# Layer-0 attention output with the head dimension on partitions: four-quadrant values, norm sums by a product with ones, norm applied behind the output product

## The chip, the cores and the metric

The kernel runs on one NeuronCore of a Trainium2 chip. The core has TensorE (PE, matrix products; its weight loads are listed as PEld), VectorE (DVE), ScalarE (ACT), GpSimd (POOL) and SyncE (SP, which issues most DMAs), each working through its own instructions in order. The metric is the device time of one execution in microseconds, lower is better; the median of several executions is compared.

## The reference

x is 64 sequences of 32 tokens with 256 features. Two layers each do x = x + attention(conditioning(x)) and x = x + mlp(conditioning(x)). The change lies in layer 0's attention, which has 16 heads of 128 (H, DK, DV) and 64 memory slots per head (M):

```python
A = jnp.where(mask, jnp.einsum('bhtd,bhjd->bhtj', q, k) * scale, 0.0)
ok = enz * jnp.einsum('bhtj,bhjm->bhtm', A, es)
qv = jax.nn.softmax(ok, axis=-1)
W2 = jnp.where(mask, jnp.einsum('bhtm,bhjm->bhtj', qv * enz, es), 0.0)
o = jnp.einsum('bhtj,bhjd->bhtd', W2, v)
o_n = o * jax.lax.rsqrt(jnp.mean(o * o, axis=-1, keepdims=True) + EPS) * g_norm_weight
o_g = o_n * (g * jax.nn.sigmoid(g))
return o_g.reshape(B, T, H * DV) @ Wo.T
```

q, k, v and g are projections of the conditioned tokens, with rotary embedding on q and k; es is exp of the clipped slot logits and enz the reciprocal of its running sum.

## The kernel before

The attention runs as a software pipeline over 32 steps: four groups of four heads (hq) times eight groups of 256 tokens (q, eight sequences each). `turn(n)` writes out by hand, once per n from -1 to 33, the order in which the pieces of neighbouring steps are issued, and this order is the order on every engine. In turn n, step n+1 gets its slot exponentials (`slots_exp`), rotated queries and keys (`project_qk`, two pairs of heads, the second pair later in the turn) and running sums (`cumsum`); step n gets `scores`, `attend`, `weigh`, the value and gate projections (`project_vg`) and `turn_qe`; step n-1 gets `mix`, `values`, `norm`, `gate` and `turn_og`; and step n-2 gets `leave`.

Lines that matter here: line 779 is the q/k projection on TensorE. Lines 790 and 791 multiply it on DVE with cosine and sine into the tiles ra and rb, and lines 793 and 794 combine these on POOL into qT and kT. Line 841 is the slot logits, 843 their exp on ACT, 848 the clip on DVE. Line 889 is the scores, 896 their mask on DVE (tile aT). Line 910 is the attend product, 918 gives `ok` on DVE, 923 its maximum, 927 the softmax exponentials on ACT. Line 864 is the running sum and 873 its reciprocal on DVE. Line 936 is `qe` = qv * enz on POOL, 950 its turning by TensorE (transposes against an identity), 954 the copy of it on ACT. Line 967 is `mix` and 975 its mask on DVE (tile w2T).

The output side: `values` (line 992) has 64 tokens on partitions and 128 columns of d in each product, two heads' parity in two PSUM banks (po). Line 1001 squares each head's 128 columns on ACT and sums them (eight instructions, each followed by an accumulator read). `norm` adds the epsilon term on DVE (line 1008) and raises to the power -1/2 on POOL (line 1010). `gate` (line 1022, eight DVE instructions) multiplies by the norm factor, a number per partition, and by Silu(g). `turn_og` (line 1032, eight transposes on TensorE, copied by ACT at lines 1036 and 1039) brings d onto the partitions, and `leave` (line 1047) multiplies with Wo, the four heads adding up in PSUM, and line 1052 adds the result to x. The epsilon term e2 is made by DVE at line 943 in `weigh`.

PSUM has eight banks, all from one pool; a product waits until the bank that it is given has been read out. Most work tiles have two buffers, some one.

Beside the attention the loop carries other work. `ahead()`, called twice in a turn, takes the next step of `preparing`: rounding the last layers' weights on DVE (lines 226 to 240 for f1, f3 and f2, then lines 196 to 204 for thirteen rows) alternating with short steps that turn the rounded rows on TensorE (line 256). `tabulating` issues table gathers on POOL (line 433). The wo weights of each head group are scaled on DVE (line 687) every eighth turn. The later stages (layer 0's mlp and layer 1, chunk by chunk) follow the loop; the first of their chunks is woven into the last turns by `more`.

Of the kernel before, what the change touches and what calls it, by code (L numbers as in the profile page):

```python
# [9 lines left out]
F32 = mybir.dt.float32  # L10
I32 = mybir.dt.int32
AF = mybir.ActivationFunctionType
ALU = mybir.AluOpType
AX = mybir.AxisListType

P = 128
B = 64
T = 32
D = 256
# [57 lines left out]
def mk_kernel(  # L77
# [10 lines left out]
    nc = tc.nc  # L88
    MULT, ADD, SUB, MAX, MIN = ALU.mult, ALU.add, ALU.subtract, ALU.max, ALU.min
# [5 lines left out]
    def bank():  # L95
        return psum.tile([P, 512], F32, tag="ps", name="ps")
# [11 lines left out]
    ident = const("ident")  # L108


    xq = [keep.tile([P, 2, D], F32, tag=f"x{q}", name=f"x{q}") for q in range(8)]
# [23 lines left out]
    ones = keep.tile([P, P], F32, tag="ones", name="ones")  # L135
    mhalf = keep.tile([P, 8], F32, tag="mhalf", name="mhalf")
# [511 lines left out]
    with ExitStack() as s1:  # L648
        p1 = s1.enter_context(tc.tile_pool(name="p1", bufs=1))
        work = s1.enter_context(tc.tile_pool(name="work", bufs=2))  # L650
# [117 lines left out]
        def at(i):  # L768
            hq, q = steps[i]
            return hq, q, weights[hq], hsT[q // 2], (q % 2) * 256, state[i]  # L770
# [30 lines left out]
        def by_parity(ap):  # L801
            return ap.rearrange("p (r e d) -> p r e d", r=2, e=2)

        def project_vg(i, which):
            hq, q, w, hs, lo, s = at(i)
            wt = w[2 if which == "v" else 3]
            for gi in range(2):
                ps = bank()
                for c in range(2):
                    nc.tensor.matmul(  # L810
                        ps, lhsT=hs[:, c, lo + gi * P : lo + (gi + 1) * P], rhs=wt[:, c, :],
                        start=(c == 0), stop=(c == 1),
                    )
                t = work.tile([P, 512], F32, tag=which, name=which, bufs=2)
                if which == "v":
                    nc.scalar.copy(t, ps)
                else:
                    to, of = by_parity(t), by_parity(ps)
                    nc.scalar.activation(to[:, :, 0, :], of[:, :, 0, :], AF.Silu)
                    for half in range(2):  # L820
                        here, there = slice(half * 64, half * 64 + 64), slice(64 - half * 64, P - half * 64)
                        nc.scalar.activation(to[here, :, 1, :], of[there, :, 1, :], AF.Silu)
                s[which, gi] = t

        E32 = float(np.exp(np.float32(32.0)))

# [23 lines left out]
        def quarters(product):  # L850


            for e in range(2):
                for at in range(2):
                    out = at ^ e
                    product(e, slice(64 * at, 64 * at + 64), slice(64 * out, 64 * out + 64))
# [76 lines left out]
        def weigh(i):  # L933
            s = state[i]
            qe = work.tile([P, 512], F32, tag="qe", name="qe", bufs=1)
            nc.gpsimd.tensor_tensor(
                qe.rearrange("p (k e m) -> p e k m", k=4, e=2),
                s["qv"].rearrange("p (e k) m -> p e k m", e=2),
                s["enz"].rearrange("p e (k m) -> p e k m", k=4), MULT,
            )  # L940

            e2 = work.tile([P, 8], F32, tag="e2", name="e2")
            nc.vector.scalar_tensor_tensor(e2, s["rs"], 1e-5, s["rs"], MULT, MULT)
            s["qe"], s["e2"] = qe, e2

        def turn_qe(i):
# [32 lines left out]
            s["w2T"] = w2T  # L979

        def values(i):
            s = state[i]
            f = work.tile([P, 8], F32, tag="f", name="f")
            s["f"] = f
            po = [bank(), bank()]
            s["po"] = po
            for k in range(4):
                gi, pr = k // 2, k % 2

                def product(e, rows, out):  # L990
                    h = pr * 2 + e
                    nc.tensor.matmul(  # L992
                        po[e][out, k * P : (k + 1) * P], lhsT=s["w2T"][rows, e, k, :],
                        rhs=s["v", gi][rows, h * P : (h + 1) * P], start=True, stop=True,
                    )

                quarters(product)
            for e in range(2):
                for k in range(4):
                    sq = work.tile([P, P], F32, tag="sq", name="sq", bufs=1)  # L1000
                    nc.scalar.activation(  # L1001
                        sq, po[e][:, k * P : (k + 1) * P], AF.Square,
                        accum_out=f[:, e * 4 + k : e * 4 + k + 1],
                    )

        def norm(i):
            s = state[i]
            nc.vector.scalar_tensor_tensor(s["f"], s["f"], 1.0 / P, s["e2"], MULT, ADD)  # L1008
            f2 = work.tile([P, 8], F32, tag="f2", name="f2")
            nc.gpsimd.tensor_tensor(f2, s["f"], mhalf, ALU.pow)  # L1010
            s["f2"] = f2

        def gate(i):

            s = state[i]
            f2 = s["f2"]
            for gi in range(2):
                s["og", gi] = work.tile([P, 4, P], F32, tag="og", name="og")
            for k in range(4):
                for e in range(2):  # L1020
                    gi, h = k // 2, k % 2 * 2 + e
                    nc.vector.scalar_tensor_tensor(
                        s["og", gi][:, h, :], s["po"][e][:, k * P : (k + 1) * P],
                        f2[:, e * 4 + k : e * 4 + k + 1], s["g", gi][:, h * P : (h + 1) * P], MULT, MULT,
                    )

        def turn_og(i):
            s = state[i]
            for gi in range(2):
                ps = bank()  # L1030
                for h in range(4):
                    nc.tensor.transpose(ps[:, h * P : (h + 1) * P], s["og", gi][:, h, :], ident)  # L1032
                t = work.tile([P, 4, P], F32, tag="ogT", name="ogT")
                to = t.rearrange("p (r e) t -> p r e t", e=2)
                of = ps.rearrange("p (r e t) -> p r e t", r=2, e=2)
                nc.scalar.copy(to[:, :, 0, :], of[:, :, 0, :])
                for half in range(2):
                    here, there = slice(half * 64, half * 64 + 64), slice(64 - half * 64, P - half * 64)
                    nc.scalar.copy(to[:, :, 1, here], of[:, :, 1, there])
                s["ogT", gi] = t  # L1040

        def leave(i):
            hq, q, w, hs, lo, s = at(i)
            ps = bank()
            for gi in range(2):
                for h in range(4):
                    nc.tensor.matmul(  # L1047
                        ps[:, gi * D : (gi + 1) * D], lhsT=s["ogT", gi][:, h, :], rhs=w[4][:, h, :],
                        start=(h == 0), stop=(h == 3),
                    )  # L1050
            xf = xq[q].rearrange("p g f -> p (g f)")
            nc.vector.tensor_tensor(xf, ps, xf, ADD)
            s.clear()

        def turn(n):

            def on(i, f, *a):
                if 0 <= i < len(steps):
                    f(i, *a)

            def more(*at):

                if n in at:
                    next(beyond)

            def ahead():
                if 2 <= n < len(steps):
                    next(preparing, None)

            N = len(steps)  # L1070
            on(n + 1, slots_exp)
            on(n, scores)
            more(N)
            on(n - 1, mix)
            on(n + 1, slots_clip)
            more(N - 1)
            on(n - 2, leave)
            more(N - 1)
            on(n + 1, project_qk, "q", 0)
            on(n + 1, project_qk, "k", 0)  # L1080
            if n < 2:
                condition(n + 2)
            on(n - 1, values)
            on(n, attend)
            on(n + 1, cumsum)
            more(N)
            on(n - 1, norm)
            on(n + 1, project_qk, "q", 1)
            on(n + 1, project_qk, "k", 1)
            on(n - 1, gate)  # L1090
            on(n, weigh)
            on(n, project_vg, "v")
            on(n, project_vg, "g")
            if n < 2:
                low_rank(n + 2)
            if n < 1:
                gather_cond(n + 3)
            if n == 1:
                small_tables()
            ahead()  # L1100
            more(N - 1)
            on(n, turn_qe)
            on(n - 1, turn_og)
            more(N)
            ahead()

# [570 lines left out]
```

## Time and profile before

| | |
|---|---|
| median of 3 runs | 1453.79 us (1450.05 to 1453.99) |
| the profiled execution's own time | 1451.43 us |
| its span | 1449.7 us |
| granted TensorE clock, mean | 0.992 |
| attention loop (first slot logits to last output product) | about 22 to 834 us |
| a turn of the loop, steady state | 23.34 to 23.62 us |

A page of the profile gives busy times, then the chain of work that ended last, followed back from the last instruction, then groups of instructions by line. A row of a group names the tile written and the tiles read, partitions x elements, how often, the busy time and the mean time of one, and the idle time of the engine before them with what ended it. A TensorE product in fp32 appears as two records, a transpose as one.

### The profile page before, as it was taken

The page shows a single profiled execution, that of the slowest core. Times are in us where ns is not written, and L with a number is a line of the kernel's source. Part 1 is how long each engine was busy: PE and PEld are TensorE (multiplying, and loading weights), DVE is VectorE, ACT ScalarE, POOL GpSimd, SP SyncE. Part 2 cuts the span into 40 slices and gives each one's busy share as a digit, 9 for nine tenths or more (in the row PEclk, how much of TensorE's full clock was granted, in tenths as well). Part 3 has the DMA queues.
Part 4 walks back from the last instruction along what each step waited for, and adds up shares of the span by engine and source line. Part 5 has one row for each costly group of instructions (what it writes and reads, how often), then busy time and mean ns, then how long its engine had stood idle before and what let it go on. Part 6 is the DMA issues. An engine that isn't in the chain of part 4 may idle for free.

```text
span 1449.7 us, 39390 instructions
## 1 busy us (share of the span) xinstructions
PE 1399.7 (97%) x16552; PEld 1086.2 (75%) x16552; DVE 829.9 (57%) x1879; ACT 614.1 (42%) x2014; POOL 577.2 (40%) x650
## 2 busy tenths in 40 slices
PE   5899999999999999999999999999999999999996
PEld 3666777776767677767777788888887878788874
DVE  1566686867677776766565323363636262635554
ACT  1355665656575756565655512130312121212121
POOL 3423367777533333333445141524251606060320
PEclk9999999999999999999999999999999999999999
DMA  6201001321221000100001161313131304040220
GB/s 172 61 2 67 5 16 20 77 47 33 35 66 36 23 6 15 38 12 1 13 14 44 38 115 52 98 49 92 39 102 34 107 17 123 6 116 23 67 74 15
DMA packets 101625, 71.41 MB, mean 49 GB/s; under 512 B 71429, under 2 KB 88965, under 8 KB 101449
## 3 DMA queue, kind: packets, MB, share of 16 engines
q0 software_dynamic: 15744, 38.03, 9.5%
q1 hardware_dynamic: 82504, 26.34, 7.6%
q10 hardware_dynamic: 3200, 4.52, 1.0%
q8 instruction: 131, 2.15, 0.6%
q14 instruction: 46, 0.37, 0.1%
HBM read 64.54 MB, written 6.29 MB: 49 GB/s over the span
## 4 chain that ended last, share of the span: by engine, by line
PE 91%; DMA 3%; SPq 2%; DVE 2%; issue 1%; ACT 1%; POOL 0%; ACTq 0%; DVEq 0%
PE ps L779 16%; PE ps L810 15%; PE ps L1047 8%; PE ps L507 8%; PE ps L1398 5%; PE ps L578 4%; PE ps L553 3%; PE ps L1438 3%; PE ps L597 3%; PE ps L992 2%; PE ps L521 2%; PE ps L889 2%; PE ps L1206 2%; PE ps L1032 2%; SPq L276 1%; PE ps L967 1%
## 5 line engine op out<-in xcount | busy, mean ns | idle before, releaser
L433 POOL DMA_INDIRECT we<-in_ew,at x64 | 61.1, 955 | 277.5 <-DVE h L1405 203.7
L1001 ACT ACTIVATE sq<-ps 128x128 f32<-128x128 f32 x256 | 71.1, 278 | 211.6 <-PE ps L992 204.4
L793 POOL TENSOR_TENSOR qT<-ra,rb 128x256 f32<-128x256 f32 x64 | 46.6, 728 | 272.6 <-DVE rb L791 272.5
L1047 PE MATMUL ps<-wo,ogT 128*128 128x256 f32 x512 | 120.6, 389 | 6.1 <-DVE aT L896 6.1
L779 PE MATMUL ps<-hsT,wq 128*128 128x256 f32 x512 | 126.4, 390 | 0.0
L779 PE MATMUL ps<-hsT,wk 128*128 128x256 f32 x512 | 122.2, 382 | 0.0
L790 DVE TENSOR_TENSOR ra<-ps,ct 128x512 f32<-128x512 f32 x128 | 87.4, 683 | 49.9 <-PE ps L779 44.9
L810 PE MATMUL ps<-wv,hsT 128*128 128x512 f32 x256 | 115.2, 593 | 0.0
L810 PE MATMUL ps<-wg,hsT 128*128 128x512 f32 x256 | 115.1, 592 | 0.0
L1047 PEld LDWEIGHTS ps<-wo,ogT 128*128 128x128 f32 x512 | 95.8, 192 | 20.9 <-DVE aT L896 6.6
L779 PEld LDWEIGHTS ps<-hsT,wq 128*128 128x128 f32 x512 | 95.5, 192 | 18.3 <-issue 5.8
L873 DVE RECIPROCAL enz<-ps 128x256 f32<-128x256 f32 x64 | 107.5, 1721 | 2.7 <-PE ps L864 2.7
L779 PEld LDWEIGHTS ps<-hsT,wk 128*128 128x128 f32 x512 | 98.3, 192 | 13.7
L1010 POOL TENSOR_TENSOR f<-f,mhalf 128x8 f32<-128x8 f32 x32 | 53.1, 1660 | 133.5 <-DVE f L1008 133.5
L810 PEld LDWEIGHTS ps<-wg,hsT 128*128 128x128 f32 x256 | 48.6, 190 | 61.2 <-issue 54.3
L791 DVE TENSOR_TENSOR rb<-ps,ct 128x512 f32<-128x512 f32 x128 | 87.0, 680 | 0.0
L927 ACT ACTIVATE qv<-ok,nmx 128x64 f32<-128x64 f32 x256 | 85.0, 336 | 1.3 <-DVE nmx L923 1.3
L810 PEld LDWEIGHTS ps<-wv,hsT 128*128 128x128 f32 x256 | 48.6, 190 | 47.6 <-issue 45.9
L1398 PE MATMUL ps<-guT,y3T 128*128 128x352 f32 x256 | 79.5, 464 | 0.5 <-ACT y3T L395 0.5
L529 DVE TENSOR_TENSOR hT<-ps,sg 128x256 f32<-128x256 f32 x64 | 24.2, 419 | 96.9 <-ACT sg L528 96.9
L896 DVE SCALAR_TENSOR_TENSOR aT<-ps,ct 128x256 f32<-128x256 f32 x64 | 24.1, 419 | 85.6 <-PE ps L889 85.6
L433 POOL DMA_INDIRECT ag<-alora,at x56 | 53.4, 954 | 49.3 <-DVE at L431 39.3
(233 smaller groups left out, 3056.4 us busy)
## 6 DMA issues: line engine op xcount, KB each, us to landing
x<-in_x SPq DMA_DIRECT2D x8, 256.0 KB
wq<-in_wqT SPq DMA_DIRECT2D x16, 128.0 KB
wk<-in_wkT SPq DMA_DIRECT2D x16, 128.0 KB
wv<-in_wvT SPq DMA_DIRECT2D x4, 512.0 KB
wg<-in_wgT SPq DMA_DIRECT2D x4, 512.0 KB
wo<-in_woT SPq DMA_DIRECT2D x4, 512.0 KB
row<-in_wgu ACTq DMA_DIRECT2D x11, 128.0 KB
out<-res SPq DMA_DIRECT2D x5, 256.0 KB
```

The lines of the kernel that those rows point to most:

```text
L433: nc.gpsimd.indirect_dma_start(out=to, out_offset=None, in_=table, in_offset=bass.IndirectOffsetOnAxis(ap=at, axis=0))
L507: nc.tensor.matmul(ps[:, i * 256 : (i + 1) * 256], lhsT=mlp[name, k // 4][:, j, part], rhs=c["xT"][:, j, :], start=(i == 0 and j == 0), st ...
L578: nc.tensor.matmul(ps[:, i * 256 : (i + 1) * 256], lhsT=wt[:, j, k * P : (k + 1) * P], rhs=yT[:, j, :], start=(j == 0), stop=(j == 1),)
L779: nc.tensor.matmul(ps[:, half * 256 : (half + 1) * 256], lhsT=wt[:, c, half * 256 + pr * P : half * 256 + (pr + 1) * P], rhs=hs[:, c, lo : ...
L790: nc.vector.tensor_tensor(by_t(a.rearrange("p h t -> p (h t)")), by_t(ps), cosb, MULT)
L791: nc.vector.tensor_tensor(by_t(b.rearrange("p h t -> p (h t)")), by_t(ps), sinb, MULT)
L810: nc.tensor.matmul(ps, lhsT=hs[:, c, lo + gi * P : lo + (gi + 1) * P], rhs=wt[:, c, :], start=(c == 0), stop=(c == 1),)
L873: nc.vector.reciprocal(t[:, e, :], banks[e][:, :256])
L927: nc.scalar.activation(qv[:, k, :], ok[:, k, :], AF.Exp, bias=nmx[:, k : k + 1], accum_out=rs[:, k : k + 1],)
L1001: nc.scalar.activation(sq, po[e][:, k * P : (k + 1) * P], AF.Square, accum_out=f[:, e * 4 + k : e * 4 + k + 1],)
L1047: nc.tensor.matmul(ps[:, gi * D : (gi + 1) * D], lhsT=s["ogT", gi][:, h, :], rhs=w[4][:, h, :], start=(h == 0), stop=(h == 3),)
L1398: nc.tensor.matmul(ps[:, :352], lhsT=c["y3T"][:, k, gi * P : (gi + 1) * P], rhs=guT[:, k, lo : lo + 352], start=(k == 0), stop=(k == 1),)
```

## The change

The values come out with d on partitions: the product takes v as the stationary operand (64 values of j by 64 of d) and w2T as the moving one, in four 64x64 quadrants, 32 products instead of 16. The gate is projected with d on partitions too, so that `turn_og` goes. The norm's sum over d is now a sum over partitions: ACT squares the values (two instructions), TensorE multiplies the squares by a tile of ones, a sequence's 32 tokens at a time into a column quarter, and DVE turns the 32x32 blocks so that the sums stand on the token's partition. As the norm factor belongs to the token, it is applied behind the output product: each head's product stays apart, and eight DVE instructions add factor times product to x. `gate` moves ahead of the second q/k pair in a turn, `norm` to the turn's end, and e2 goes from DVE to ACT.

```diff
-        def project_vg(i, which):
-            ...
+        def project_v(i):
+            ...
+        def project_g(i):
+            hq, q, w, hs, lo, s = at(i)
+            g = work.tile([P, 4, 256], F32, tag="g", name="g", bufs=1)
+            for pr in range(2):
+                ps = bank()
+                for e in range(2):
+                    h = pr * 2 + e
+                    for c in range(2):
+                        nc.tensor.matmul(
+                            ps[:, e * 256 : (e + 1) * 256], lhsT=w[3][:, c, h * P : (h + 1) * P],
+                            rhs=hs[:, c, lo : lo + 256], start=(c == 0), stop=(c == 1),
+                        )
+                nc.scalar.activation(
+                    g[:, pr * 2 : pr * 2 + 2, :].rearrange("p e t -> p (e t)"), ps, AF.Silu
+                )
+            s["g"] = g
...
-            e2 = work.tile([P, 8], F32, tag="e2", name="e2")
-            nc.vector.scalar_tensor_tensor(e2, s["rs"], 1e-5, s["rs"], MULT, MULT)
+            e2 = work.tile([P, 2, 2, 2], F32, tag="e2", name="e2")
+            rs = s["rs"].rearrange("p (e g r) -> p e g r", e=2, g=2)
+            nc.scalar.activation(e2[:, :, :, 0], rs[:, 0], AF.Square, scale=1e-5**0.5)
+            for half in range(2):
+                here, there = slice(half * 64, half * 64 + 64), slice(64 - half * 64, P - half * 64)
+                nc.scalar.activation(e2[here, :, :, 1], rs[there, 1], AF.Square, scale=1e-5**0.5)
+            e2 = e2.rearrange("p g r e -> p (g r e)")
...
         def values(i):
             s = state[i]
...
             po = [bank(), bank()]
             s["po"] = po
...
+            for gi in range(2):
+                for h in range(4):
+                    for half in range(2):
+                        rows = slice(64 * half, 64 * half + 64)
+                        k = gi * 4 + h
+                        for d in range(2):
+                            nc.tensor.matmul(
+                                po[half][d * 64 : (d + 1) * 64, k * 64 : (k + 1) * 64],
+                                lhsT=s["v", gi][rows, h * P + d * 64 : h * P + (d + 1) * 64],
+                                rhs=s["w2T"][rows, h % 2, gi * 2 + h // 2, :], start=True, stop=True,
+                            )
+            sq = work.tile([P, 8, 2, 64], F32, tag="sq", name="sq", bufs=1)
+            for half in range(2):
+                nc.scalar.activation(
+                    sq[:, :, half, :], po[half].rearrange("p (k t) -> p k t", k=8), AF.Square
+                )
+            s["sq"] = sq
...
         def norm(i):
             s = state[i]
+            ps = bank()
+            for b in range(4):
+                nc.tensor.matmul(
+                    ps[32 * b : 32 * b + 32, :256].rearrange("p (k t) -> p k t", k=8), lhsT=ones[:, :32],
+                    rhs=s["sq"].rearrange("p k a t -> p k (a t)")[:, :, b * T : (b + 1) * T],
+                    start=True, stop=True,
+                )
+            sums = s["sq"].rearrange("p k a t -> p (k a t)")[:, :256]
+            nc.vector.transpose(sums, ps[:, :256])
+            f = work.tile([P, 8], F32, tag="f", name="f")
+            nc.vector.scalar_tensor_tensor(f, sums.rearrange("p (k t) -> p k t", k=8)[:, :, 0], 1.0 / P, s["e2"], MULT, ADD)
             f2 = work.tile([P, 8], F32, tag="f2", name="f2")
...
         def gate(i):
             s = state[i]
+            og = work.tile([P, 4, 256], F32, tag="og", name="og", bufs=1)
+            to = og.rearrange("p h (g a t) -> p a g h t", g=2, a=2)
+            by = s["g"].rearrange("p h (g a t) -> p a g h t", g=2, a=2)
+            for half in range(2):
+                nc.vector.tensor_tensor(
+                    to[:, half], s["po"][half].rearrange("p (g h t) -> p g h t", g=2, h=4), by[:, half], MULT
+                )
+            s["og"] = og
...
-        def turn_og(i):
-            ...
         def leave(i):
             hq, q, w, hs, lo, s = at(i)
+            for gi in range(2):
+                for pr in range(2):
+                    ps = bank()
+                    for e in range(2):
+                        h = pr * 2 + e
+                        nc.tensor.matmul(
+                            ps[:, e * D : (e + 1) * D], lhsT=s["og"][:, h, gi * P : (gi + 1) * P],
+                            rhs=w[4][:, h, :], start=True, stop=True,
+                        )
+                    for e in range(2):
+                        of = gi * 4 + pr * 2 + e
+                        nc.vector.scalar_tensor_tensor(
+                            xq[q][:, gi, :], ps[:, e * D : (e + 1) * D], s["f2"][:, of : of + 1],
+                            xq[q][:, gi, :], MULT, ADD,
+                        )
             s.clear()
...
             on(n + 1, cumsum)
             more(N)
-            on(n - 1, norm)
+            on(n - 1, gate)
             on(n + 1, project_qk, "q", 1)
             on(n + 1, project_qk, "k", 1)
-            on(n - 1, gate)
             on(n, weigh)
-            on(n, project_vg, "v")
-            on(n, project_vg, "g")
+            on(n, project_v)
+            on(n, project_g)
...
             on(n, turn_qe)
-            on(n - 1, turn_og)
+            on(n - 1, norm)
             more(N)
             ahead()
```

## The prediction

> **What bounds the kernel now.** I read the page first (busy shares, then the chain that ended last), then busy time by stretch, and then, since TensorE looked saturated, the timeline of one turn of the layer-0 attention loop engine by engine, to see how much room the other engines have in that turn.
>
> ```profile
> PE 1399.7 (97%) x16552; PEld 1086.2 (75%) x16552; DVE 829.9 (57%) x1879; ACT 614.1 (42%) x2014; POOL 577.2 (40%) x650
> PE 91%; DMA 3%; SPq 2%; DVE 2%; issue 1%; ACT 1%; POOL 0%; ACTq 0%; DVEq 0%
> 652.00:791.70 139.70, 139.70 (x1558) 102.80 (x1557) 88.13 (x176) 87.18 (x318) 65.64 (x75) 1.00 0.06 17
> ```
>
> The third line is a stretch by engine (PE, PEld, DVE, ACT, POOL): from 652 to 791.7 us PE is never idle. By these views TensorE is the bound and only TensorE time counts. The next view, one turn of the steady state (its output product, line 1047, starts at 675.31, the next one at 698.65, so the turn lasts 23.34), says how close the second is. Columns: start, length, engine, line, operation.
>
> ```profile
> 684.02 0.75 DVE L918 TENSOR_TENSOR ok<-ps,enz 128x256 f32<-128x256 f32 x2 [0.15 <-PE ps L910]
> 685.41 3.36 DVE L873 RECIPROCAL enz<-ps 128x256 f32<-128x256 f32 x2
> 688.68 0.10 DVE L1008 SCALAR_TENSOR_TENSOR f<-f,e 128x8 f32<-128x8 f32 x1
> 688.70 0.68 DVE L790 TENSOR_TENSOR ra<-ps,ct 128x512 f32<-128x512 f32 x1
> 690.49 0.68 DVE L791 TENSOR_TENSOR rb<-ps,ct 128x512 f32<-128x512 f32 x1
> 691.09 2.15 DVE L1022 SCALAR_TENSOR_TENSOR og<-ps,f,g 128x128 f32<-128x128 f32 x8
> 698.02 0.76 DVE L896 SCALAR_TENSOR_TENSOR aT<-ps,ct 128x256 f32<-128x256 f32 x2 [4.71 <-PE ps L889]
> ...
> 688.87 1.65 POOL L1010 TENSOR_TENSOR f<-f,mhalf 128x8 f32<-128x8 f32 x1 [3.44 <-DVE f L1008]
> 690.49 0.73 POOL L793 TENSOR_TENSOR qT<-ra,rb 128x256 f32<-128x256 f32 x1
> 693.23 1.27 POOL L936 TENSOR_TENSOR qe<-qv,enz 128x512 f32<-128x512 f32 x1
> ...
> 694.78 0.60 PE L950 MATMUL ps<-ct,qe 128*128 128x128 f32 x4
> 695.21 1.04 PE L1032 MATMUL ps<-ct,og 128*128 128x128 f32 x8
> 696.18 0.48 PE L841 MATMUL ps<-ws,rT 17*128 17x256 f32 x2
> 697.81 0.91 PE L967 MATMUL ps<-qeT,es 64*64 64x64 f32 x32
> 698.65 1.13 PE L1047 MATMUL ps<-wo,ogT 128*128 128x256 f32 x4
> ```
>
> A second chain runs beside TensorE: the attend product gives `ok` (684.02), then the reciprocals, then on DVE ra and rb of the second q/k pair, then four rotations on POOL, then `qe` on POOL (ends 694.50), whose turning is TensorE's line 950 at 694.78. TensorE had been busy until just then, so this chain has no room left: the answer for tile `qe` lists the wait below. In those turns the weight load follows `qe`'s end by 0.05 us and the matmul by 0.24 us.
>
> ```profile
>   POOL qe L936: 6.0, 13
> ```
>
> 13 of 32 turns already wait for POOL, 0.46 us each on the weight load. The last view is DVE in an earlier turn, one in which a weight row is rounded for the last layer (rows 196 to 204): the rounding lies in DVE's pause before aT, 2.05 us of it with its waits, and hides there:
>
> ```profile
> 453.33 0.41 DVE L196 TENSOR_REDUCE qs<-row 128x1 f32<-128x256 f32 x1
> 455.11 0.35 DVE L204 TENSOR_SCALAR row<-row,qs 128x256 f32<-128x256 f32 x1
> 458.34 0.76 DVE L896 SCALAR_TENSOR_TENSOR aT<-ps,ct 128x256 f32<-128x256 f32 x2 [2.21 <-PE ps L889]
> ```
>
> **What the Trainium skill says.** "VectorE: DVE Perf Modes", section on the TRN2 errata: an fp32 tensor_tensor takes (N+151)/0.96 ns. The trace agrees: 690 to 692 ns at N=512, 419 at 256, with starts 0.60 apart back to back. Same page, "The three transpose paths": DVE turns 32x32 blocks only, which is why the sums come in column quarters; STREAM_TRANSPOSE of 1024 columns took 1245 ns here, so I take the same formula for 256, 0.43 us. "TensorE: Matmul & The Clock Gate", Part 3: column tiles on different strips run together. The trace agrees: line 1368 (128 rows, 32 columns, 256 wide) starts four within 0.02 us and four more every 0.216 us. "TensorEngine Tiling (Array Packing)", Key Properties: a change of tiling mode drains the array. Here the output product begins 0.15 us after the last 64x64 matmul issues.
>
> **The change on TensorE.** A plain turn, sums in us. Turning og goes: line 1032 to line 841, 0.97. The norm's four fp32 products (eight records, two rounds of 0.22 to 0.24, and a drain of about 0.12) cost 0.57. So after line 950 TensorE saves 0.40. Before line 950: gate projection, 8 records of 512 columns at 0.430 (3.44) become 16 of 256 at 0.216 to 0.228 (3.45 to 3.65); values, 32 records in 0.92 become 64 at the scores' 0.058 per four, 0.93 plus drain, +0.05. Output product: 16 records before and after. Net on TensorE alone: -0.35 to -0.15 per turn.
>
> **The change on DVE and POOL, where I put the outcome.** `gate` now stands ahead of the second q/k pair in code order, and POOL's `qe` stands behind that pair's rotations. From `ok`, in the same turn's clock:
>
> - `ok` 0.05 later (values): 684.07. Reciprocals unchanged, so DVE is free at 688.73.
> - gate, two tensor_tensor of 128x512 from PSUM, by row L790: 0.61 apart, 1.22. Next is ra at 689.95, last rb at 691.75, against 690.49 now. The small f (0.02) leaves this place.
> - POOL: the power (1.65) leaves too; it now holds the first rotation until 690.49, 0.34 later than rb (ends 689.97, plus 0.17) would allow. New first rotation: rb ends 691.22, plus 0.17, 691.39. Four at 0.685, `qe` 694.13 to 695.40.
> - TensorE's line 950: 0.24 later, 695.64, against 694.78: +0.86. The 0.25 dearer gate and values projections lie inside this wait.
> - Then the 0.40 saved: next turn +0.46, period 23.80 instead of 23.34.
>
> **What I cost at nothing, and its cover.** `leave`: one 0.69 add becomes eight scalar_tensor_tensor in a row on one x tile, each waiting for the one before. Row L1339 has this form, 479 ns; 0.035 more for the wait (spacing of the rounding's dependent operations, 454.78 after 454.75): 8 x 0.514 = 4.11. They start after the clip. The exps now start 0.15 after the mix instead of 0.65 because six copies of ogT leave ACT, so the clip ends at +2.1 from the output product; eight end at +6.1; ra, rb, ra, rb to +8.5; TensorE's attend delivers at +8.7. Covered by 0.2 to 0.3 us; at 0.60 each the cover is gone and each turn loses 0.4 more. The four banks come from aT and w2T, emptied before TensorE needs them. e2's three small ACT operations, the two squares instead of eight (each 278 plus 194 ns now), and ACT's Silu of 128x512 instead of three pieces: ACT waits 1 us for v behind them. The power on POOL now sits after `qe` and ahead of the table gathers; those end about 4 us later, at +11.4, the first pair's rotations at +14.3, and the second ra needs their buffer at +14.6. No DMA is added; the SP copies behind the gathers move 4 us.
>
> **What moves.** DVE's norm operations now come after `turn_qe`, and the second preparing step of a turn (a row's rounding, or a reduction) comes after them instead of straight after gate. Norm's products end at 696.71, the transpose 697.18, f about 697.3; the row's 2.05 us end at 699.35, where aT could start at 698.48. The output product follows a late aT by 0.46 (as at 316.6, where a turn took 24.34): 699.81 against 699.11, +0.70 in each row turn. In these turns the row's own transposes (0.28 of TensorE) hide in the wait for `qe`: 24.50 against 23.62, +0.88.
>
> **The sum.** From the output product at 127.88, which a DMA (f1T, landed 125.74) re-times in both kernels: that turn +0.4; eight turns to 340.94, 188.0 now, 8 x 23.80 + 0.32 (a reduction of 1.67) + 0.93 (one with the wo scaling behind) + 0.70 = 192.35, +4.3; ten row turns 8.8, plus 0.7 for a wo scaling; the first 704-wide row (2.97 of DVE) +1.8; the two turns with the DMA of the second -0.5; five plain turns +2.3; the last ones, bound by TensorE, -0.3. Sum +17.5. Later stages are the same instructions. 1451.43 + 17.5 = 1468.9; the median stands 2.36 above the profiled execution, so 1471.
>
> **Rivals.**
>
> A, this forecast: TensorE waits for `qe`. 1462 to 1481 with gate at 1.1 to 1.4, norm 0.45 to 0.75, a row's delay 0.4 to 0.9. 0.70.
>
> B, `leave` uncovers: the eight dependent operations at 0.60 or more make `ok` late. For: cover of only 0.3. Against: row L1339 is the same form. 1480 to 1495. 0.09.
>
> C, balance: gate's operations overlap more or POOL catches up, and the delay is about the 0.40 that TensorE saves; rows fit. 1449 to 1459. 0.10.
>
> D, faster: TensorE stays the bound and pockets its 0.15 to 0.35 in about 30 turns, and 1 us of ACT copies gone keeps mix fed: 1440 to 1449, 1446 at 0.25. For: the page's 97%. The place is line 950, the price 0.86: it decides if the gate costs under 0.4 instead of 1.22. Against: two reads of 512 columns from PSUM, 0.69 each everywhere. 0.11.
>
> 0.3% (4.4 us) is about what a measurement can tell from no change. Slower: A, B and a little of C, 0.79; same 0.09; faster 0.12. A's own range is 1462 to 1481; for eight in ten I take in C and the edge of B, 1450 to 1483.
>
> **What would show it.** Right: line 965 (turning qe) waiting for POOL qe in nearly all turns, 0.6 us each; a plain turn of 23.8, a row turn of 24.5; the output product waiting for aT in row turns; PE's share below 97% while its busy time falls. Wrong: plain turns of 23.1 (D); `ok` waiting for DVE's ra/rb instead of TensorE (B); gate's pair under 0.6 in all.

## The result and the profile after

The changed kernel takes 1470.87 us (median of six runs, 1468.22 to 1472.91) where the kernel before takes 1451.78 (six runs, 1448.60 to 1453.99): ratio 1.0139, 95% interval 1.0126 to 1.0151. It is slower by some 19 us. The forecast was 1471. The profiled execution took 1468.55 us, 17.1 more than that of before; the forecast worked out 17.5.

The page of the changed kernel, busy time by engine and then the shares of the chain that ended last:

```profile
PE 1391.9 (95%) x17832; PEld 1108.1 (76%) x17832; DVE 897.1 (61%) x1911; ACT 499.5 (34%) x1342; POOL 581.5 (40%) x650
PE 70%; DVE 15%; POOL 7%; issue 4%; DMA 2%; ACT 1%; SPq 1%; POOLq 0%; ACTq 0%; DVEq 0%
```

TensorE is busy 7.8 us less than before (1399.7), and the kernel is slower. The chain says why: DVE's share has gone from 2% to 15%, POOL's from nothing to 7%. TensorE no longer bounds the loop alone.

One plain turn of the loop by timeline. The output product, line 1059 (before: 1047), starts at 689.56 and again at 713.12, so the turn lasts 23.56. DVE first, then POOL, then TensorE; columns are start, length, engine, line, operation, and in brackets the idle time and who ended it. Rows between the ones shown are left out here and in the timelines below.

```profile
698.33 0.75 DVE L928 TENSOR_TENSOR ok<-ps,enz 128x256 f32<-128x256 f32 x2 [0.27 <-PE ps L920]
703.00 1.22 DVE L1046 TENSOR_TENSOR og<-ps,g 128x512 f32<-128x512 f32 x2
704.14 0.68 DVE L790 TENSOR_TENSOR ra<-ps,ct 128x512 f32<-128x512 f32 x1
705.93 0.68 DVE L791 TENSOR_TENSOR rb<-ps,ct 128x512 f32<-128x512 f32 x1
712.64 0.76 DVE L906 SCALAR_TENSOR_TENSOR aT<-ps,ct 128x256 f32<-128x256 f32 x2 [1.05 <-PE ps L899]
...
705.58 0.73 POOL L793 TENSOR_TENSOR qT<-ra,rb 128x256 f32<-128x256 f32 x1 [5.84 <-DVE rb L791]
707.64 0.73 POOL L794 TENSOR_TENSOR kT<-ra,rb 128x256 f32<-128x256 f32 x1
708.32 1.27 POOL L946 TENSOR_TENSOR qe<-qv,enz 128x512 f32<-128x512 f32 x1
...
709.65 0.66 PE L965 MATMUL ps<-ct,qe 128*128 128x128 f32 x4 [0.38 <-POOL qe L946]
710.23 0.64 PE L1026 MATMUL ps<-sq,ones 128*32 128x256 f32 x8
713.12 0.70 PE L1059 MATMUL ps<-wo,og 128*128 128x256 f32 x2
```

This is the forecast chain, link by link. `gate` (line 1046) takes 1.22 us ahead of ra; POOL idles until rb is there; its four rotations and `qe` follow without a gap; TensorE has run out of work and stands still for the turning of `qe` (line 965). The 0.27 at `ok` is the cover of `leave`: DVE is done with everything else by then and waits for TensorE.

A row turn (a weight row is rounded in it), DVE and then TensorE; its output product came at 538.42 and the next at 562.65, 24.23 later:

```profile
560.28 0.17 DVE L1034 SCALAR_TENSOR_TENSOR f<-sq,e 128x8 f32<-128x8 f32 x1
560.36 0.41 DVE L196 TENSOR_REDUCE qs<-row 128x1 f32<-128x256 f32 x1
561.91 0.35 DVE L204 TENSOR_SCALAR row<-row,qs 128x256 f32<-128x256 f32 x1
562.18 0.75 DVE L906 SCALAR_TENSOR_TENSOR aT<-ps,ct 128x256 f32<-128x256 f32 x2
...
562.65 1.13 PE L1059 MATMUL ps<-wo,og 128*128 128x256 f32 x4 [0.72 <-DVE aT L906]
```

The rounding now starts behind norm's f (560.28) and ends where aT should have started. aT has no idle time in front of it, and TensorE waits 0.72 us. The views of the tiles `qe` and `aT` in the changed kernel, who waited for each (us in total, times):

```profile
  PEld ps L965: 18.0, 27
  PE ps L965: 9.8, 25
...
  PEld ps L1059: 20.4, 28
  PE ps L1059: 16.0, 16
```

Before, TensorE's weight load waited for `qe` 13 times, 6.0 us, and for `aT` 4 times, 6.6 us; its product (line 950) never waited for `qe`.

### The profile page after: what moved, and what is told of

Read it like the earlier page. It is cut to its first block, busy times and chain, and to the rows that moved or that the text cites. A ratio compares the mean times of both kernels' runs of the same rounds, so it can differ in the third digit from the quotient of the medians.

```text
span 1466.8 us, 41124 instructions
## 1 busy us (share of the span) xinstructions
PE 1391.9 (95%) x17832; PEld 1108.1 (76%) x17832; DVE 897.1 (61%) x1911; ACT 499.5 (34%) x1342; POOL 581.5 (40%) x650
## 4 chain that ended last, share of the span: by engine, by line
PE 70%; DVE 15%; POOL 7%; issue 4%; DMA 2%; ACT 1%; SPq 1%; POOLq 0%; ACTq 0%; DVEq 0%
PE ps L779 9%; PE ps L1059 8%; PE ps L507 8%; PE ps L578 5%; PE ps L1413 5%; PE ps L553 4%; DVE enz L883 3%; PE ps L1453 3%; PE ps L597 3%; PE ps L1008 2%; POOL qe L946 2%; PE ps L521 2%; PE ps L1221 2%; DVE og L1046 2%; PE ps L809 2%
## 5 line engine op out<-in xcount | busy, mean ns | idle before, releaser
L1059 PE MATMUL ps<-wo,og 128*128 128x256 f32 x512 | 123.8, 396 | 16.6 <-DVE aT L906 16.0
L1065 DVE SCALAR_TENSOR_TENSOR x<-ps,f,x 128x256 f32<-128x256 f32 x256 | 120.9, 482 | 14.6 <-PE ps L1059 3.3
L1059 PEld LDWEIGHTS ps<-wo,og 128*128 128x128 f32 x512 | 98.0, 196 | 33.6 <-DVE aT L906 20.4
L826 PEld LDWEIGHTS ps<-hsT,wg 128*128 128x128 f32 x512 | 97.3, 190 | 26.9 <-issue 15.3
L826 PE MATMUL ps<-hsT,wg 128*128 128x256 f32 x512 | 115.7, 379 | 0.0
L1015 ACT ACTIVATE sq<-ps 128x512 f32<-128x512 f32 x64 | 34.8, 595 | 234.1 <-PE ps L1008 229.6
L1032 DVE STREAM_TRANSPOSE sq<-ps 128x256 f32<-128x256 f32 x32 | 14.4, 450 | 126.1 <-PE ps L1026 126.1
L1036 POOL TENSOR_TENSOR f<-f,mhalf 128x8 f32<-128x8 f32 x32 | 56.9, 1778 | 85.4 <-DVE f L1034 85.4
```

The costliest lines, as they stand in the source:

```text
L826: nc.tensor.matmul(ps[:, e * 256 : (e + 1) * 256], lhsT=w[3][:, c, h * P : (h + 1) * P], rhs=hs[:, c, lo : lo + 256], start=(c == 0), stop ...
L1059: nc.tensor.matmul(ps[:, e * D : (e + 1) * D], lhsT=s["og"][:, h, gi * P : (gi + 1) * P], rhs=w[4][:, h, :], start=True, stop=True,)
L1065: nc.vector.scalar_tensor_tensor(xq[q][:, gi, :], ps[:, e * D : (e + 1) * D], s["f2"][:, of : of + 1], xq[q][:, gi, :], MULT, ADD,)
```

## The experiments

All are timed against the kernel before on the same chip (1451.3 us for gate_late, prep_early, both_moved and half_adds, 1450.72 for weigh_early and the three with spaced rows). Two waits stand to be told apart, then `leave`, then what is left.

**gate_late: gate back behind the second q/k pair.**

```diff
-            on(n - 1, gate)
             on(n + 1, project_qk, "q", 1)
             on(n + 1, project_qk, "k", 1)
+            on(n - 1, gate)
```

> The changed kernel with gate back behind the second q/k pair, norm left where the change put it. Theory (the second chain, DVE gate ahead of ra/rb, then POOL, sets the turn): the matmul of line 965 no longer waits for POOL qe, a plain turn falls from 23.56 to about 23.0, a row turn from 24.24 to about 23.9 (there aT behind the rounding still binds), the whole to about 1460. Rival (TensorE's own smaller products, 16 gate projections and 32 values products, made the turn longer): turns unchanged, 1471.

Measured: 1456.72 us, ratio 1.0043 (1.0028 to 1.0058). A plain turn takes 22.96, a row turn 23.86. POOL and then TensorE in a plain turn that begins at 680.81:

```profile
697.70 0.72 POOL L794 TENSOR_TENSOR kT<-ra,rb 128x256 f32<-128x256 f32 x1
698.38 1.27 POOL L946 TENSOR_TENSOR qe<-qv,enz 128x512 f32<-128x512 f32 x1
...
696.90 3.62 PE L826 MATMUL ps<-hsT,wg 128*128 128x256 f32 x16
700.36 0.60 PE L965 MATMUL ps<-ct,qe 128*128 128x128 f32 x4
```

`qe` ends at 699.65, 0.7 us before TensorE comes to it; line 965 has no idle time in front of it. By the view of tile `qe`, TensorE's weight load waits for it once in the whole run, 0.2 us. The theory held, and the rival fell: the place of gate costs 14 us (1470.9 to 1456.7), the larger part of the loss. The waits for aT stay as they were (28 times, 20.6 us).

**weigh_early: qe ahead of the second q/k pair's rotations, gate where the change put it.** This asks whether gate's 1.22 us is lost as DVE time, or only through the rotations that stand ahead of `qe` in POOL's queue.

```diff
+            on(n, weigh)
             on(n + 1, project_qk, "q", 1)
             on(n + 1, project_qk, "k", 1)
-            on(n, weigh)
```

> The changed kernel with one call moved: weigh (qe on GpSimd) ahead of the second q/k pair, gate left where the change put it. Theory (it is the order of GpSimd's queue that makes TensorE wait; gate's pair does it only by pushing the rotations that stand ahead of qe): qe no longer depends on the rotations, ends near 15 us into the turn, and TensorE's turning of qe has no wait left. A plain turn of 22.96 us as with gate moved back, row turns of 23.86 (aT still waits behind the row's rounding), the whole near 1457 us. Rival (gate's pair costs DVE time that comes out somewhere whatever the order): the plain turn stays above 23.3, with the wait moved to the second pair's rotations or to the next turn's scores, the whole above 1463.

Measured: 1455.86 us, ratio 1.0040 (1.0029 to 1.0052); plain turn 22.96, row turn 23.86, the same as gate_late to 0.01 us. POOL in a plain turn:

```profile
692.58 1.27 POOL L946 TENSOR_TENSOR qe<-qv,enz 128x512 f32<-128x512 f32 x1 [3.06 <-ACT qv L937]
695.37 0.73 POOL L793 TENSOR_TENSOR qT<-ra,rb 128x256 f32<-128x256 f32 x1 [1.52 <-DVE rb L791]
697.42 0.72 POOL L794 TENSOR_TENSOR kT<-ra,rb 128x256 f32<-128x256 f32 x1
```

gate still stands ahead of ra on DVE and the rotations are as late as in the changed kernel, yet nothing is lost: they are wanted only in the next turn. The wait came through the order of POOL's queue, and gate's DVE time by itself costs nothing here.

**prep_early: the second preparing step ahead of norm.**

```diff
             on(n, turn_qe)
-            on(n - 1, norm)
             ahead()
+            on(n - 1, norm)
```

> The changed kernel with the second preparing step of a turn taken ahead of norm instead of behind it, gate left where the change put it. Theory: the output product no longer waits for aT in row turns, which fall from 24.24 to about 23.56 to 23.9 (the rounding may slow POOL's rotations beside it), plain turns stay 23.56, the whole about 1462. Rival (the row turns are longer because of their own transposes on TensorE): row turns stay within 0.2 of 24.24, 1470.

Measured: 1462.76 us, ratio 1.0082 (1.0060 to 1.0103). Row turns 23.66, plain turns 23.56 as before the edit. Who waited for `qe`, and then for `aT`:

```profile
  PEld ps L965: 21.6, 27
  PE ps L965: 13.5, 27
...
  PEld ps L1059: 4.8, 26
```

The wait for aT is as good as gone (20.4 us on the weight load and 16.0 on the product became 4.8 and none listed). The one for `qe` stays, and grows: 18.0 to 21.6 on the weight load, 9.8 to 13.5 on the product. So moving the rounding back from behind norm gains 8 us net, and the two waits can be removed one without the other.

**both_moved: gate_late and prep_early together.**

> The changed kernel with both moves, gate behind the second q/k pair and the second preparing step ahead of norm. Theory: both waits gone, TensorE is the bound with the 0.40 us a turn that norm saves against turning og: plain turns about 23.0, row turns about 23.25, the whole about 1441, faster than the kernel before. Rival (the eight dependent operations of leave hold DVE back): plain turns stay at 23.3 or more and ok waits for DVE, 1450 or more.

Measured: 1445.76 us, ratio 0.9971 (0.9962 to 0.9979): faster than the kernel before. Plain turns 22.96, row turns 23.18, against 23.34 and 23.62 before. The 25 us that the two moves give back together are 3 more than the sum of each alone (14.2 and 8.1). This agrees with prep_early, which alone gives back 3.7 us in longer waits of line 965 for `qe`; with gate moved too, that wait is gone. But it missed the expectation by 5 us, and two turns hold these: the ones in which the last two weight rows (704 wide, one buffer) are done, 27.85 and 25.57 us. Stretches in this place; the columns are the stretch, its length, PE, PEld, DVE, ACT, POOL busy (instructions), the granted clock, DMA:

```profile
612.00:618.50 6.50, 3.21 (x92) 2.16 (x90) 3.01 (x7) 3.12 (x6) 0.00 (x0) 0.88 0.17 55
618.50:625.00 6.50, 6.20 (x43) 5.15 (x44) 4.77 (x12) 1.21 (x4) 1.65 (x1) 0.59 0.01 3
```

TensorE stands still for half of the first stretch: DVE waits for the row's transfer, norm's transpose stands behind the rounding, and TensorE waits for that. It then runs at a granted clock of 0.59 for the next.

**half_adds: half of leave's additions left out** (the products of every second head are computed and not added, so half of the attention's output is missing from x).

```diff
-                    for e in range(2):
+                    for e in range(1):
```

> The changed kernel with only every other one of leave's eight DVE operations, so half of the heads' products is left out of x. DVE does about 2 us less a turn. Theory (leave is covered): plain and row turns and the whole unchanged within 0.2 percent, 1470. Rival (leave's dependent operations make ok late): turns shorter by 0.3 or more, 1461 or less.

Measured: 1469.81 us, ratio 1.0123 (1.0101 to 1.0145). Plain turn 23.56, row turn 24.24, nothing moved. DVE in a plain turn:

```profile
699.49 0.69 DVE L790 TENSOR_TENSOR ra<-ps,ct 128x512 f32<-128x512 f32 x1 [0.44 <-PE ps L779]
700.10 0.68 DVE L791 TENSOR_TENSOR rb<-ps,ct 128x512 f32<-128x512 f32 x1
701.05 0.76 DVE L928 TENSOR_TENSOR ok<-ps,enz 128x256 f32<-128x256 f32 x2 [0.27 <-PE ps L920]
```

DVE now waits for TensorE before ra already, 0.44 us, and `ok` still comes 0.27 after rb, released by TensorE. Four dependent operations fewer buy nothing: `leave` is covered, and rival B falls.

**Spaced rows: the second 704-wide row rounded one turn after its load**, in both_moved, in the changed kernel, and in the kernel before:

```diff
             r = pool.tile([P, 1], F32, tag="qr", name="qr")
+            if k == 12:
+                yield
+                yield
             yield
             largest(s, r, t)
```

> Both steps moved (gate behind the second q/k pair, the preparing step ahead of norm), and the second 704-wide row rounded one turn after its load instead of in the turn of its load. Theory (in the two turns after the first 704 row TensorE stands still for this row's transfer, its clock falls after the idle time, and that is the whole of what they cost): 27.85 + 25.57 + 22.96 us become 23.4 + 23.2 + 23.4, 6 us less, no slice below full clock there, the whole near 1440 us. Rival (the 704-wide row's own rounding and five transposes cost this): the loss moves one turn on, the whole stays at 1446 us.

> The changed kernel with only the second 704-wide row rounded one turn later. Theory: 28.64 + 25.05 + 23.56 us become 23.56 + 25.41 + 23.56 (the row's own 1.8 us stays, for here it delays aT), 4.7 us less: 1466 us. Rival: 1471 us, the loss one turn on.

> The kernel before with only the second 704-wide row rounded one turn later. Theory: 26.86 + 24.39 + 23.34 us become 23.8 + 23.6 + 23.8, 3.4 us less: 1448 us, ratio 0.9977. So of the loss of the change about 1.3 us (4.7 less 3.4) lies in a wait for a transfer that both kernels have, made dearer. Rival: 1451 us, as before.

Measured: both_moved_spaced 1440.43 us, ratio 0.9937 (0.9913 to 0.9962); after_spaced 1469.58, ratio 1.0128 (1.0102 to 1.0154); before_spaced 1449.22, ratio 0.9981 (0.9972 to 0.9990). With both steps moved, the theory held: the three turns 27.85, 25.57, 22.96 became 23.62, 22.96, 23.62, and the stretch behind the second row runs at full clock:

```profile
640.50:646.00 5.50, 5.50 (x26) 4.87 (x27) 4.79 (x12) 1.21 (x4) 0.59 (x1) 1.00 0.00 0
```

In the changed kernel it failed: the four turns from the first 704 row on went from 25.41, 28.64, 25.05, 23.56 to 25.40, 25.30, 26.07, 25.31, only 0.6 us less in all where 4.7 was expected. What I had overlooked is in after_spaced's timeline, two output products and their waits:

```profile
614.55 0.70 PE L1062 MATMUL ps<-wo,og 128*128 128x256 f32 x2 [1.89 <-DVE aT L909]
...
665.92 0.85 PE L1062 MATMUL ps<-wo,og 128*128 128x256 f32 x2 [2.55 <-DVE aT L909]
```

and in the stretch that follows the first of them:

```profile
614.60:618.50 3.90, 3.90 (x11) 3.14 (x12) 3.09 (x8) 0.00 (x0) 0.00 (x0) 0.57 0.02 6
```

No transfer is late here. The 704-wide row's own rounding, behind norm, holds aT up for 1.9 us, and for 2.6 where a wo scaling follows it, and the granted clock behind these waits is 0.57 and 0.56; `ok` then comes 10.46 us into both turns instead of 8.77, another 1.7 us. So in the changed kernel each 704 row costs twice, its wait and the slow clock after it, and the rival I had set down ("the loss one turn on") was nearly right. In the kernel before, the turns of 26.86, 24.39 and 23.34 us became 24.39, 23.34 and 24.39, 2.5 us less where 3.4 was expected. (A 704-wide row has six transposes, not the five of the expectation.)

## Why the prediction was right

The time was right, and so was its mechanism; some terms were mis-sized and happened to cancel. That 1471 was met to a few tenths of a microsecond is luck: it was reckoned from a median of before that six runs put 2.0 us lower (1451.78 instead of 1453.79), and the medians differ by 19.1, not 17.5. By the prediction's own steps:

**TensorE saves 0.40 behind line 950, and little before it.** Right. From the turning of `qe` to the output product it is 3.47 us (709.65 to 713.12) against 3.87 before. Where nothing waits (gate_late), a whole turn is 22.96 against 23.34: 0.38. In the kernel before, TensorE's products do not wait in a plain turn either, so this is a saving of TensorE's own. Rival D's mechanism is therefore real, and larger than the 0.15 to 0.35 I gave it; only the order of the queues hid it.

**gate's pair makes qe late.** Right, and by the predicted way. Worked out, `qe` runs from 18.82 to 20.09 into the turn; measured 18.76 to 20.03 (708.32 less 689.56). What failed is the last link, "line 950: 0.24 later": TensorE's matmul follows `qe`'s end by 0.06 us, not 0.24. So +0.62 at line 965 instead of +0.86, a plain turn of 23.56 instead of 23.80, a row turn of 24.24 instead of 24.50. The 0.24 was read in a turn of before in which TensorE still had work when `qe` ended: its last product of line 810 runs to 694.94, past the start of line 950. This term was overestimated by a quarter of a microsecond in every turn.

**The norm's operations delay a row's rounding, and that delays aT.** Right: +0.68 for a row turn over a plain one (24.24 less 23.56), predicted +0.70. prep_early took 8 us away with this one edit. The DVE transpose in front of it was estimated at 0.43 us by the tensor_tensor formula of the Trainium skill ("VectorE: DVE Perf Modes", section on the TRN2 errata), which exactly worked out gives 0.42; it measured 0.45.

**leave is covered by 0.2 to 0.3.** Right: 0.27 in the timeline, and half_adds changed nothing. The additions measured 482 ns each, worked out as 479 from another row.

**The sum.** In the profile, by turns; measured is the difference between the two kernels:

| part | predicted | measured |
|---|---|---|
| up to the output product that followed f1T's transfer, and the turn after | +0.4 | -3.25 |
| eight turns with reductions and gathers | +4.3 | +5.9 |
| ten row turns | +9.5 | +7.1 |
| first 704-wide row | +1.8 | +1.8 |
| the two turns with the second row's transfer | -0.5 | +2.4 |
| five plain turns | +2.3 | +1.1 |
| last turns | -0.3 | 0.0 |
| later stages | 0 | +1.9 |
| all | +17.5 | +17.1 |

The first and last of these lines are not put down to the change. Ten profiles are at hand: the third output product lies anywhere from 149.7 to 152.9 us, by when the first transfers land, and from the start of the last output product to the end it is 619.6 to 622.2 with the same instructions; the kernel before and before_spaced, which differ by one delayed row, span 2.6 of that between them. From the third to the last output product, where only the loop counts, it is 677.1 before and 695.6 after: +18.4, of which I had 17.1. The overestimate of the plain and row turns (3.6 us) was more than made good by two terms I had too small:

- The eight turns, 1.6 too small. A preparing operation now runs on DVE beside POOL's rotations, which stand on the chain, and there the rotation takes longer. In the turn that begins at 149.68, DVE and then POOL:

```profile
166.65 0.89 DVE L240 TENSOR_SCALAR f<-f,tsc 128x768 f32<-128x768 f32 x1
...
166.39 0.73 POOL L794 TENSOR_TENSOR qT<-ra,rb 128x256 f32<-128x256 f32 x1
167.08 1.04 POOL L793 TENSOR_TENSOR kT<-ra,rb 128x256 f32<-128x256 f32 x1
```

  1.04 instead of 0.73 us, and `qe` 0.3 later for it. Six of the eight turns have one such rotation, 1.9 us in all. The ten profiles bear this out: all 33 rotations of the loop that began while DVE ran a TENSOR_SCALAR of 128x768 took 1.04 to 1.05 us, and all 60 that had begun before it came took 0.71 to 0.74. gate_late and both_moved have none of the first kind, prep_early has nine.

- The turns with the second 704 row, 2.9 too small. "The two turns with the DMA of the second -0.5" took it that the transfer would swallow the delay. Instead TensorE's idle time grew and its clock fell twice. In the changed kernel's timeline, two output products with their waits:

```profile
612.30 0.92 PE L1059 MATMUL ps<-wo,og 128*128 128x256 f32 x3 [1.89 <-DVE aT L906]
640.95 0.79 PE L1059 MATMUL ps<-wo,og 128*128 128x256 f32 x1 [3.39 <-DVE aT L906]
```

  and three stretches, the first with the wait of 1.89, the others behind the two waits (first number behind the comma: PE busy; third from the end: clock):

```profile
609.74:613.15 3.41, 1.52 (x52) 1.30 (x42) 3.25 (x9) 1.21 (x4) 1.04 (x1) 1.00 0.00 0
613.15:616.56 3.41, 3.41 (x10) 2.67 (x9) 2.54 (x6) 0.00 (x0) 0.00 (x0) 0.50 0.03 7
640.46:643.87 3.41, 2.92 (x7) 2.38 (x8) 2.72 (x8) 0.00 (x0) 0.00 (x0) 0.50 0.00 0
```

  The low clock makes `ok` late by 1.69 and 1.43 us in these turns, and the longer idle time is 1.0 more than before's 2.40: 4.1 us. 1.7 of it comes back: before, a 704 row's six transposes lengthen a turn by 1.05 (24.39 against 23.34), and here they fall into TensorE's wait for `qe` (28.64 less 3.39 and 1.69 is a plain turn's 23.56). In the kernel before, the same place shows a wait and no slow clock:

```profile
627.59 0.70 PE L1047 MATMUL ps<-wo,ogT 128*128 128x256 f32 x2 [2.40 <-DVE aT L896]
```

  and the stretches in which it lies, both at full clock:

```profile
623.40:626.82 3.42, 1.71 (x92) 1.44 (x91) 2.52 (x6) 3.39 (x11) 0.00 (x0) 1.00 0.03 9
626.82:630.23 3.41, 2.65 (x12) 2.36 (x13) 2.31 (x6) 0.15 (x1) 0.00 (x0) 1.00 0.00 0
```

  Why these stretches were chosen, and why 2.40 us of waiting cost no clock here where 1.89 did there, is said in the last section.

**Rivals.** A came about, near the middle of its own range. B fell with half_adds. A plain turn lies midway between A (+0.46) and C (0, the delay equal to the 0.40 saved), at +0.22; the row turns decide for A. D describes the kernel with both steps moved and the second row spaced: 1440.43 us, 0.63% below the kernel before. Of that, spacing alone gives the kernel before 0.19%; the ratio of the medians of the two spaced kernels is 1440.43 / 1449.22 = 0.9939.

What stays open: whether moving one wait across the edge of a clock window would turn the slow clock on and off, as the last section reads it from the ten traces, and why a rotation that begins beside a preparing operation is slower.

## What to carry to other kernels

When an engine saves work, follow what the edit does to the order of the other queues before counting the gain: here 0.38 us a turn on the bound engine was lost to 1.22 us on DVE and to four POOL operations that nobody wanted yet and that stood ahead of one that TensorE was waiting for. Ask of each operation on the chain what stands ahead of it in its queue, and whether that is wanted sooner; moving two calls turned +1.4% into -0.3%. And price an idle gap of TensorE of about 2 us or more at its length plus the slow clock that may follow, 1.4 to 1.7 us here.

## What the runs showed of the hardware

**In these loops the clock followed the idle time within a window of 3.41 us.** "TensorE: Matmul & The Clock Gate" of the Trainium skill, Part 1, has the clock fall to half after an idle window of about 3.4 us, with a window that runs freely. The traces agree on the half rate and on the window. From the first output product to the last, the slow stretches in the clock record of the ten profiles all have a clock of 0.50 and last 3.41 or 6.83 us, and within a run they start whole multiples of 3.413 us apart: in the changed kernel at 125.04, 613.15 and 640.46, 143 and 8 such steps.

The traces differ from the page on how much idle time it takes. Laid out from these starts, the loops have 2141 windows. All 27 in which TensorE stood idle for 1.77 us or more were followed by a slow window, and none of the 2112 with 1.60 us or less was. One with 1.66 was and one with 1.70 was not, so about half of a window is the edge here. The changed kernel's wait of 1.89 us lay within one window (609.74 to 613.15). The wait of 2.40 us in the kernel before lay across two: 1.70 us of idle time in the first (623.40 to 626.82, 1.64 of them from this wait) and 0.77 in the second. That is the case with 1.70, and it kept full clock. The length of a wait alone therefore doesn't decide. This is read from the traces; no run moved a wait across the edge of a window. Behind the loop it isn't the whole rule: some slow windows there followed windows with 0.4 to 1.3 us of idle time.

**From POOL's end to TensorE's start.** 0.06 us when TensorE is already waiting for `qe` (POOL ends at 709.59, the matmul starts at 709.65).

**DVE and POOL side by side.** For the rotation above, the order of the starts decided in all 93 cases: it took 1.04 to 1.05 us when DVE's TENSOR_SCALAR was already running, 0.71 to 0.74 when the rotation was. A gather on POOL does not explain the like on DVE: one clip of `es` (line 858) beside a gather took 0.95 us, at 223.14, and the other eleven of the changed kernel behind the third output product that ran beside one took 0.68 to 0.70.
